# Attention scores in 32 x 64 tiles of the array, and half of the x3 tiles turned through DRAM

## The chip, the cores and the metric

The kernel runs on one core of a Trainium2 chip. The metric is the time of one execution on the device in microseconds (us). Engines are named as in the profile: PE is TensorE's matrix product, PEld its load of weights, DVE is VectorE, ACT ScalarE, POOL GpSimd; SPq, POOLq and ACTq are the queues from which transfers (DMA) are issued.

## What is computed

A block of four layers over 8 x 512 tokens of 1024 features, all in f32, each with a layer norm ahead and a residual around it:

```
x = x + softmax_attention(layernorm(x))      # 32 heads of 32 features, no mask
x = x + gated_dense(layernorm(x))            # x1 -> x2
x = x + sigmoid_attention(layernorm(x))      # 4 heads of 256 features, causal: x2 -> x3
x = x + gated_dense(layernorm(x))            # same weights as above: x3 -> out
```

In softmax attention, q, k and v come from one product with `attn_qkvw`; `probs = softmax(q @ k.T / sqrt(32))`, `ctx = probs @ v`, then a product with `attn_ow`. In sigmoid attention q, k and v are the normed x itself times a vector of signs for each, and `attn = sigmoid(4 * scores / 16)` below the diagonal. The gated dense layer is

```
dots = softmax(x @ centroids.T / 0.1); hits = dots > 0.01       # 64 clusters
out = (x @ weight.T + bias) where any(hits, axis=1) and cluster_sel[assignments], else 0
```

so it has to know the cluster logits of all tokens, and which clusters any token hit, before its output is gated.

## The kernel before, in words

Work is cut into 32 tiles of 128 tokens (four to a batch). The order on every engine is written out by hand: instructions run on each engine in the order in which the program issues them, and semaphores follow from the tiles that they read and write. Every f32 product runs on PE as two passes, so the profile has two matmul records and two weight loads for each; a bf16 product has one.

Stage 1, softmax attention, goes over 64 units (batch by group of 4 heads, the loop `for n in range(units)` from line 1002). A unit has four score steps for the maxima of the next unit (`rows_step`, product at line 871, negated maximum on DVE at 872) and four for its own exponentials (`keys_step`: product of keys and queries at 900, subtraction of the maximum as a bf16 product with ones at 903, exponential on ACT at 905). A score step writes one PSUM tile `sc` of 128 x (4 heads x 512); there is one such buffer, so rows and keys steps take turns with DVE and ACT reading it. Each head has 32 features, so its product uses 32 rows of the array: the four heads stand in four row groups, with 128 columns each. The array is then cut into tiles of 32 rows by 128 columns ("32*128" in the profile). Between score steps PE runs pieces of other work from a queue (`filler`, taken by `between`): the projections to q, k, v and the output product, cut into column tiles of 64 or 32 by `product` (line 554, "128*64" and "128*32"). Values (`values_step`, 927) and denominators (`normalize`, 939) are in 128*32.

Stage 2 is the first dense layer (line 1236), in 128*128. At its end, each pair of x2 tiles is normed and turned (features to partitions) by `block_pieces`: a block transpose of 32 x 32 on DVE (line 294), then four transfers from SP's queue (line 300) which put the blocks at their places in DRAM in pieces of 128 bytes.

Stage 3, sigmoid attention, goes over 32 heads (`for s in range(heads + 1)`). A step of this loop issues: loads of xT for head s + 2 (`load_head`, line 1275, SP's queue), the scores of head s (line 1295, `csc`), the logits by token of an earlier tile (line 333), k of the next head (line 1287, ACT), a load of an x2 tile (line 1484, SP's queue), the turn of a finished x3 tile, the norm of the next one, the values of head s - 1 (line 1314, `o`, added to x by DVE at 1320), the cluster logits of the turned tile, and what was held back (`run_held`: the steps of the cluster softmax). From step 5 on, each step finishes one x3 tile's path by one stage: norm in one step, turn and cluster logits in the next, logits by token in the one after.

The turn of an x3 tile is `turn_pieces`: eight transposes on PE against the identity (line 277) into two PSUM tiles, two copies out of PSUM (line 279, one by DVE and one by ACT), and a store of the turned tile to DRAM from GpSimd's queue (line 1442), from where the second dense layer loads it. The cluster logits are `by_cluster` (line 325, 128*64: two halves of the features in two column tiles) with a copy to `lT` by ACT (329), and `by_token` (333) after that.

Stage 4 is the second dense layer, with out stored tile by tile.

Of the kernel before, what the change touches and what calls it, by code (L numbers as in the profile page):

```python
# [13 lines left out]
F32 = mybir.dt.float32  # L14
# [8 lines left out]
P = 128  # L23
B, S, H = 8, 512, 1024
NT = B * S
NC = H // P
TPB = S // P
NTILE = NT // P
# [5 lines left out]
HEADS_B, HD_B = 4, 256  # L34
SIG_SCALE = 4.0 * HD_B ** -0.5

NCL = 64
# [31 lines left out]
class Filler:  # L69
# [38 lines left out]
    def run(self, count):  # L108

        while self.queue and count:  # L110
            count -= self._run_one() > 0
# [193 lines left out]
class Clusters:  # L305
# [8 lines left out]
    def pieces(self, t, xT, later=None, width=NCL, product=None):  # L314

        nc, (b, i), st, ps_m = self.stage.nc, divmod(t, TPB), {}, self.stage.ps_m

        def by_cluster():  # L320
            acc = ps_m.tile([P, P], F32, tag="mm", name="logitsT")
            for c in range(NC):
                for j in range(NCL // width):
                    rows = ts(c % 2 * (NCL // width) + j, width)
                    nc.tensor.matmul(  # L325
                        acc[rows, :], self.cT[:, c, ts(j, width)], xT()[:, c, :], start=(c < 2), stop=(c >= NC - 2)
                    )
            st["lT"] = self.pool.tile([P, P], F32, tag="lT", name=f"lT_{self.name}_{t}")
            nc.scalar.copy(st["lT"], acc)

        def by_token():
            acc = ps_m.tile([P, NCL], F32, tag="mm", name="logits")
            (product or nc.tensor.matmul)(acc, st["lT"], self.stage.cst.twice, start=True, stop=True)
            if i == 0:
                self.logits[b] = self.pool.tile([P, TPB, NCL], F32, tag="lg", name=f"lg_{self.name}_{b}")
            nc.scalar.activation(self.logits[b][:, i, :], acc, AF.Copy, scale=INV_TEMP)
            if i == TPB - 1:
                steps = self.softmax(b)
                if later is None:
                    for step in steps:  # L340
                        step()
                else:
                    later(steps)

        return [(1.3, by_cluster), (0.25, by_token)]

    def softmax(self, b):

        nc, small, st = self.stage.nc, self.stage.small, {}
        lg = self.logits.pop(b)  # L350

        def wide(t):
            return t.unsqueeze(2).to_broadcast([P, TPB, NCL])

        def first():
            top = small.tile([P, TPB], F32, tag="top", name="top")
            nc.vector.tensor_reduce(top, lg, AX.X, ALU.max)
            nc.vector.tensor_tensor(lg, lg, wide(top), ALU.subtract)

        def exp():  # L360
            nc.scalar.activation(lg, lg, AF.Exp)

        def second():
            den = small.tile([P, TPB], F32, tag="cden", name="cden")
            nc.vector.tensor_reduce(den, lg, AX.X, ALU.add)
            nc.vector.reciprocal(den, den)
            nc.vector.tensor_tensor(lg, lg, wide(den), ALU.mult)

        def third():
            nc.vector.tensor_scalar(lg, lg, THRESHOLD, None, ALU.is_gt)  # L370
            nc.vector.tensor_reduce(self.query[:, ts(b, TPB)], lg, AX.X, ALU.max)

        def fourth():
            turned = lg.rearrange("p t c -> p c t")
            if b == 0:
                nc.vector.tensor_reduce(self.hits, turned, AX.X, ALU.max)
            else:
                some = small.tile([P, NCL], F32, tag="some", name="some")
                nc.vector.tensor_reduce(some, turned, AX.X, ALU.max)
                nc.vector.tensor_max(self.hits, self.hits, some)  # L380

        return [first, exp, second, third, fourth]

    def rows_pieces(self, one_hot, bias, pool, out):

        nc, ps_m, st = self.stage.nc, self.stage.ps_m, {}

        def count():
            acc = ps_m.tile([NCL, P], F32, tag="mm", name="count")
            nc.tensor.matmul(acc, self.hits, self.stage.cst.ones, start=True, stop=True)  # L390
            st["sel"] = self.pool.tile([P, P], F32, tag="lT", name="cluster_sel")[:NCL]
            nc.vector.tensor_scalar(st["sel"], acc, 0.0, None, ALU.is_gt)

        def rows():
            out["rows"] = pool.tile([P, H], F32, tag="rows", name=f"rows_{self.name}")
            out["bias"] = pool.tile([P, H], F32, tag="rbias", name=f"rbias_{self.name}")
            for half in range(2):
                cols = ts(half, S)
                acc = ps_m.tile([P, S], F32, tag="mm", name="sel")
                nc.tensor.matmul(acc, st["sel"], one_hot[:, cols], start=True, stop=True)  # L400
                nc.vector.tensor_copy(out["rows"][:, cols], acc)
            nc.vector.tensor_tensor(out["bias"], out["rows"], bias, ALU.mult)

        return [(0.3, count)], [(1.7, rows)]


def softmax_attention(tc, cst, stage, filler, clusters, pools, dr, late, args):
# [11 lines left out]
    nc, small, ps_m = tc.nc, stage.small, stage.ps_m  # L419
# [45 lines left out]
    used, side, tiles, waiting, ready, held = {"w": 0}, deque(), deque(), deque(), deque(), []  # L465
# [397 lines left out]
    def rows_step(n, qt):  # L863

        st = state[n]
        if qt == 0:
            st["nmax"] = small.tile([P, TPB, GH], F32, tag="nmax", name=f"nmax_{n}")
        sc = ps_s.tile([P, GH, S], F32, tag="sc", name="sc")
        for h in range(GH):
            rows = ts(h, HD_A)  # L870
            nc.tensor.matmul(sc[:, h, :], st["q"][rows, ts(qt, P)], st["k"][rows, :], start=True, stop=True)  # L871
        nc.vector.tensor_reduce(st["nmax"][:, qt, :], sc, AX.X, ALU.max, negate=True)  # L872

    def split_max(n):
# [19 lines left out]
    def keys_step(n, kt):  # L894

        st = state[n]
        sc = ps_s.tile([P, GH, S], F32, tag="sc", name="sc")
        for h in range(GH):
            rows = ts(h, HD_A)
            nc.tensor.matmul(sc[:, h, :], st["k"][rows, ts(kt, P)], st["q"][rows, :], start=True, stop=False)  # L900
        for h in range(GH):
            rows = ts(h, HD_A)
            nc.tensor.matmul(sc[:, h, :], cst.ones_h[rows, :], st["shift"][rows, :], start=False, stop=True)  # L903
        pT = ptp.tile([P, GH, S], F32, tag="pT", name=f"pT_{n}_{kt}")
        nc.scalar.activation(pT, sc, AF.Exp, scale=SCALE_A)  # L905
        st["pT", kt] = pT
# [95 lines left out]
    for n in range(units):  # L1002
# [33 lines left out]
        for i in range(TPB):  # L1036
# [13 lines left out]
            if i == 0 and n > 0:  # L1050
                values_step(n - 1, 1)
                if ready:
                    by_cluster, by_token = ready.popleft()
# [274 lines left out]
def block_body(tc, long, dr, args, out):  # L1328
    x, xT_in, qkvw, qkvb, ow, ob, bv_q, bv_k, bv_v, wT, fbias, cT, assign = args
    nc = tc.nc  # L1330
    cst = Consts(nc, long)
# [13 lines left out]
    small, lgp, ps_m = at_left("small", 2), at_left("lg", 1), at_left("ps_m", 3, PSUM)  # L1345
    stage, filler = Stage(tc, cst, small, ps_m), Filler()
    hits1 = Clusters(stage, long, lgp, cT_s, "a")
    hits2 = Clusters(stage, long, lgp, cT_s, "b")
# [38 lines left out]
    sel, pairs = {}, NTILE // 2  # L1387
# [72 lines left out]
            turns.append((scale, stage.block_pieces(xn, xT, dr.xT2[t])))  # L1460
        return turns

    def x3_pieces(t):

        xn, xT, last = turned_tile(t, dr.xT3)
        norm = stage.norm_pieces(lambda: x2[t], xn)
        norm.insert(1, (0.0, lambda: nc.gpsimd.dma_start(dr.x3[t], x2[t])))
        later = held.extend if t < NTILE - TPB else None
        return norm, stage.turn_pieces(xn, xT, last, vector=(t < NTILE - TPB - 1)), hits2.pieces(t, xT, later)


# [55 lines left out]


    sig.open(pools(sig_stack, left))
    turned, normed, by_token = None, None, []  # L1530
    for s in range(heads + 1):
        load_head(s + 2)
        if s < heads:
            sig.scores(*divmod(s, HEADS_B))
        run(by_token)
        by_token = []
        if s + 1 < heads:
            sig.keys(*divmod(s + 1, HEADS_B))
        if s == 0:
            for t in range(2, TPB):  # L1540
                sig.value(t, x2, keep(t))
        elif s == 1:
            run([scale for scale, _ in turns])
        load_x2(s + TPB)
        turned, normed = normed, None
        if turned is not None:
            run(turned[0])
        if s > HEADS_B:
            norm, *normed = x3_pieces(s - HEADS_B - 1)
            run(norm)  # L1550
        if s > 0:
            sig.values(*divmod(s - 1, HEADS_B), x2)
        if turned is not None:
            run(turned[1][:1])
            by_token = turned[1][1:]
        run_held()
        if s in (2, 3):
            run(turns[s - 2][1])
        t = s + TPB - 1
        if TPB <= t < NTILE:  # L1560
            sig.value(t, x2, keep(t))
# [88 lines left out]
```

## Time and profile before

| what | us |
|---|---|
| median of 3 runs | 3797.39 (3795.68 to 3800.85) |
| the profiled execution | 3800.22 |
| its span, first to last instruction | 3798.5 |

By stage, from the windows of the trace (busy time, us):

| stage | window | PE | DVE | ACT | POOL | DMA share |
|---|---|---|---|---|---|---|
| first norm and projections | 0 to 70 | 58.5 | 32.9 | 6.6 | 9.8 | 0.50 |
| softmax attention | 70 to 2580 | 2484.4 | 1728.0 | 667.0 | 376.9 | 0.51 |
| end of output product, dense 1 | 2580 to 3046 | 453.0 | 362.2 | 68.3 | 42.5 | 0.66 |
| sigmoid attention | 3046 to 3392 | 341.3 | 166.7 | 156.1 | 165.4 | 0.53 |
| dense 2 | 3392 to 3798 | 398.5 | 249.4 | 18.0 | 7.6 | 0.38 |

How such lines are read: a group of instructions is "line engine operation out<-in shape xcount", then its busy time and the mean of one in ns (matmuls overlap, so count times mean is more than busy), then the idle time of the engine just before them and who ended it. "128*64" is the cut of the array: rows by columns. A line of the timeline is "start, duration, engine, line, operation", with equal instructions that follow each other merged.

### The profile page before, as it was taken

What the parts mean: (1) busy time and instruction counts of PE and PEld (TensorE: products, weight loads), DVE (VectorE), ACT (ScalarE), POOL (GpSimd) and SP (SyncE); (2) the same over time, 40 slices, a digit from 0 to 9 for tenths busy, and PEclk for the clock granted to TensorE, in tenths of its full rate; (3) what the DMA queues carried; (4) which work ended last, traced back from release to release, by engine and by line L of the source; (5) the groups of instructions that cost most, each with busy time, mean ns of one, the idle gap of its engine ahead of it and who ended that gap; (6) DMA issues with size and microseconds to landing.
All of it is one profiled execution on the core that took longest, in us unless ns stands there. A gap on an engine that the chain in (4) does not pass through costs nothing.

```text
span 3798.5 us, 72361 instructions
## 1 busy us (share of the span) xinstructions
PE 3735.7 (98%) x30850; PEld 1914.9 (50%) x30850; DVE 2539.2 (67%) x3495; ACT 916.0 (24%) x996; POOL 602.2 (16%) x585
## 2 busy tenths in 40 slices
PE   8999999999999999999999999998999999999999
PEld 4444454544554555455445445543444467764444
DVE  4767676767667666766866767665788844456556
ACT  1222222222222222222222222232111144430000
POOL 1222111111111111111111111111000045530000
PEclk9999999999999999999999999999999999999999
DMA  5335455645655455465465454456566765543332
GB/s 169 114 126 170 130 144 148 191 137 146 189 145 146 151 174 149 131 198 148 131 182 152 144 149 121 120 158 226 155 177 177 188 178 193 193 186 133 128 133 100
DMA packets 674544, 591.47 MB, mean 156 GB/s; under 512 B 268072, under 2 KB 519984, under 8 KB 674224
## 3 DMA queue, kind: packets, MB, share of 16 engines
q1 hardware_dynamic: 645120, 482.77, 44.3%
q0 software_dynamic: 24784, 88.36, 5.9%
q10 hardware_dynamic: 4320, 15.73, 1.0%
q8 instruction: 244, 4.00, 0.5%
q14 instruction: 76, 0.62, 0.0%
HBM read 452.48 MB, written 134.25 MB: 154 GB/s over the span
## 4 chain that ended last, share of the span: by engine, by line
PE 90%; DVE 7%; issue 1%; DMA 1%; ACT 0%; POOL 0%; SPq 0%; DVEq 0%; ACTq 0%; POOLq 0%
PE mm L554 39%; PE dense L1236 19%; PE sc L900 7%; PE sc L871 7%; PE av L927 6%; PE csc L1295 4%; PE o L1314 4%; DVE nmax L872 2%; PE logitsT L325 1%; PE sc L903 1%; PE den L939 1%; PE tp L277 1%; DVE sum L916 1%; DVE ln_st L227 0%; DVE xT L534 0%
## 5 line engine op out<-in xcount | busy, mean ns | idle before, releaser
L872 DVE TENSOR_REDUCE nmax<-sc 128x4 f32<-128x2048 f32 x256 | 586.0, 2289 | 298.5 <-PE sc L871 298.5
L905 ACT ACTIVATE pT<-sc 128x2048 f32<-128x2048 f32 x256 | 480.8, 1878 | 1147.5 <-PE sc L903 1136.4
L554 PE MATMUL mm<-xT,w 128*64 128x256 f32 (+1 forms) x3736 | 429.4, 384 | 1.8 <-DVE rden L942 1.7
L914 POOL TENSOR_TENSOR sum<-pT,pT 128x1024 f32<-128x1024 f32 x128 | 309.7, 2443 | 753.4 <-ACT pT L905 712.2
L554 PEld LDWEIGHTS mm<-xT,w 128*64 128x64 f32 (+1 forms) x3736 | 242.2, 135 | 198.6 <-issue 46.5
L554 PE MATMUL mm<-s,w 128*32 128x256 f32 (+1 forms) x3672 | 321.3, 381 | 3.9 <-DVE qk L144 3.4
L900 PE MATMUL sc<-qk,qk 32*128 32x512 f32 x2048 | 294.0, 644 | 17.2 <-DVE nmax L872 16.4
L871 PE MATMUL sc<-qk,qk 32*128 32x512 f32 x2048 | 294.8, 640 | 0.5 <-ACT pT L905 0.3
L916 DVE TENSOR_TENSOR sum<-sum,pT 128x2048 f32<-128x2048 f32 x128 | 292.0, 2281 | 1.0 <-ACT pT L905 1.0
L142 DVE TENSOR_TENSOR u<-dense,u 128x512 f32<-128x512 f32 x223 | 149.2, 686 | 183.9 <-PE dense L1236 167.0
L554 PEld LDWEIGHTS mm<-s,w 128*32 128x32 f32 (+1 forms) x3672 | 179.9, 122 | 180.8 <-issue 64.2
L554 PE MATMUL mm<-ow,ctxT 128*32 128x512 f32 (+2 forms) x1276 | 246.4, 599 | 0.8 <-DMA ow<-o_T 0.8
L927 PE MATMUL av<-pT,v 128*32 128x512 f32 x2048 | 246.6, 599 | 0.0
L1236 PE MATMUL dense<-sum,s 128*128 128x512 f32 x512 | 232.2, 594 | 2.6 <-DVE s L1183 2.6
L554 PEld LDWEIGHTS mm<-w,xT 128*64 128x64 f32 (+1 forms) x3888 | 197.5, 133 | 57.2 <-issue 44.7
L554 PE MATMUL mm<-w,xT 128*64 128x128 f32 (+1 forms) x3888 | 218.1, 274 | 0.0
L144 DVE SCALAR_TENSOR_TENSOR qk<-mm,qkvb_s,qk 128x256 f32<-128x256 f32 x224 | 107.6, 480 | 123.7 <-PE mm L554 118.7
L554 PE MATMUL mm<-ow,c 128*64 128x512 f32 (+2 forms) x864 | 171.1, 597 | 2.8 <-DMA ow<-o_T 2.8
L1236 PE MATMUL dense<-wT_s,dT_b 128*128 128x512 f32 x384 | 171.4, 594 | 1.6 <-DMA dT_b<-xT 1.6
L1236 PE MATMUL dense<-wT_s,dT_a 128*128 128x512 f32 x384 | 171.1, 594 | 0.0
L554 PE MATMUL mm<-w,s 128*64 128x128 f32 x2688 | 162.5, 274 | 0.0
L1236 PEld LDWEIGHTS dense<-sum,s 128*128 128x128 f32 x512 | 96.6, 190 | 123.2 <-issue 111.9
(230 smaller groups left out, 4548.4 us busy)
## 6 DMA issues: line engine op xcount, KB each, us to landing
w<-in_qkvw SPq DMA_DIRECT2D x252, 256.0 KB, 3.0
ow<-o_T SPq DMA_DIRECT2D x240, 256.0 KB, 3.7
w<-qk_T SPq DMA_DIRECT2D x224, 256.0 KB, 2.8
ow<-in_ow SPq DMA_DIRECT2D x180, 256.0 KB, 3.2
w<-v_T SPq DMA_DIRECT2D x112, 256.0 KB, 2.7
x<-in_x SPq DMA_DIRECT2D x32, 512.0 KB, 4.6
dT_a<-xT SPq DMA_DIRECT2D x32, 512.0 KB, 6.1
x_a<-x SPq DMA_DIRECT2D x32, 512.0 KB, 6.7
```

The costliest lines, as they stand in the source:

```text
L142: nc.vector.tensor_tensor(out, acc, other, ALU.add)
L554: nc.tensor.matmul(out[cols], lhsT[:, cols], rhs, **flags)
L871: nc.tensor.matmul(sc[:, h, :], st["q"][rows, ts(qt, P)], st["k"][rows, :], start=True, stop=True)
L872: nc.vector.tensor_reduce(st["nmax"][:, qt, :], sc, AX.X, ALU.max, negate=True)
L900: nc.tensor.matmul(sc[:, h, :], st["k"][rows, ts(kt, P)], st["q"][rows, :], start=True, stop=False)
L905: nc.scalar.activation(pT, sc, AF.Exp, scale=SCALE_A)
L914: nc.gpsimd.tensor_tensor(st["sum"][:, h, :], st["pT", 0][:, h, :], st["pT", 1][:, h, :], ALU.add)
L916: nc.vector.tensor_tensor(st["sum"], st["sum"], st["pT", kt], ALU.add)
L927: nc.tensor.matmul(st["av"][rows, :], st["v"][:, kt, rows], pT[:, h, :], start=(kt == 0), stop=(kt == TPB - 1))
L1236: nc.tensor.matmul(st["acc"], st["left"][LEFT[k]][:, c, :], self.w[RIGHT[k]][:, c, :], start=(c == 0), stop=(c == half - 1),)
L1295: nc.tensor.matmul(sc[:, AT_OFF[i] : AT_OFF[i] + n], k[:, c, ts(i, P)], xT[:, c, i * P :], start=(c == 0), stop=(c == 1),)
L1314: nc.tensor.matmul(acc[:, j - jj, :], at[:, start : start + P], self.v[b * TPB + i][:, cols], start=(i == 0), stop=(i == j),)
```

## The change

Three edits that can be told apart, and one of space:

1. Scores. In `rows_step` and `keys_step` each head's product of 128 columns becomes two of 64, which write the lower and the upper 64 partitions of the same place in `sc`; the product of the maxima with ones likewise. The array is then cut 32*64, in eight tiles. Products per rows step: 8 for 4; per keys step: 8 f32 and 8 bf16 for 4 and 4.
2. x3's even tiles, 0 to 24 (13 tiles), are turned by `block_pieces` in place of `turn_pieces`: the block transpose on DVE and its four sends from SP's queue are put behind what is held at the end of the step that normed the tile; in the next step a fetch from SP's queue brings the turned tile back from DRAM.
3. The cluster logits of an even tile then wait for those of the next odd tile, and both run one behind the other; so do their logits by token, one step later.
4. `lT` gets two buffers (`lT0`, `lT1`) for this, and the little tile `some` moves to another pool with one buffer in place of two.

```diff
@@ Clusters @@
-            st["lT"] = self.pool.tile([P, P], F32, tag="lT", name=f"lT_{self.name}_{t}")
+            st["lT"] = self.pool.tile([P, P], F32, tag=f"lT{t % 2}", name=f"lT_{self.name}_{t}")
...
-                some = small.tile([P, NCL], F32, tag="some", name="some")
+                some = self.pool.tile([P, NCL], F32, tag="some", name="some")
...
-            st["sel"] = self.pool.tile([P, P], F32, tag="lT", name="cluster_sel")[:NCL]
+            st["sel"] = self.pool.tile([P, P], F32, tag="lT0", name="cluster_sel")[:NCL]
@@ rows_step @@
-            nc.tensor.matmul(sc[:, h, :], st["q"][rows, ts(qt, P)], st["k"][rows, :], start=True, stop=True)
+            for j in range(2):
+                cols = ts(2 * qt + j, P // 2)
+                nc.tensor.matmul(sc[ts(j, P // 2), h, :], st["q"][rows, cols], st["k"][rows, :], start=True, stop=True)
@@ keys_step @@
-            nc.tensor.matmul(sc[:, h, :], st["k"][rows, ts(kt, P)], st["q"][rows, :], start=True, stop=False)
+            for j in range(2):
+                cols = ts(2 * kt + j, P // 2)
+                nc.tensor.matmul(sc[ts(j, P // 2), h, :], st["k"][rows, cols], st["q"][rows, :], start=True, stop=False)
...
-            nc.tensor.matmul(sc[:, h, :], cst.ones_h[rows, :], st["shift"][rows, :], start=False, stop=True)
+            for j in range(2):
+                cols = ts(j, P // 2)
+                nc.tensor.matmul(sc[cols, h, :], cst.ones_h[rows, cols], st["shift"][rows, :], start=False, stop=True)
@@ x3_pieces @@
-    def x3_pieces(t):
+    def x3_pieces(t, blocks=False):
...
+        if blocks:
+            made = []
+            def box():
+                if not made:
+                    made.append(Tpool.tile([P, NC, P], F32, tag="T3", name=f"B3_{t}"))
+                return made[0]
+            def fetch():
+                nc.sync.dma_start(xT().rearrange("p c t -> p (c t)"), dr.xT3[t])
+            held.extend(what for _, what in stage.block_pieces(xn, box, dr.xT3[t]))
+            return norm, [(0.0, fetch)], hits2.pieces(t, xT, later)
@@ the loop over heads @@
+    def in_blocks(t):
+        return t % 2 == 0 and t < NTILE - TPB - 3
...
-            norm, *normed = x3_pieces(s - HEADS_B - 1)
+            t = s - HEADS_B - 1
+            norm, *normed = x3_pieces(t, in_blocks(t))
...
-            run(turned[1][:1])
-            by_token = turned[1][1:]
+            clustered.append(turned[1])
+            if not in_blocks(s - HEADS_B - 2):
+                for by_cluster, _ in clustered:
+                    run([by_cluster])
+                by_token = [second for _, second in clustered]
+                clustered = []
```

`block_pieces`, which both x2's turn and this one call:

```python
def turn():
    self.nc.vector.transpose(box().rearrange("p c t -> p (c t)"), x())

def send():
    blocks = box().rearrange("p c t -> p (c t)")
    dst = dram.rearrange("(j q) (c i t) -> i q c j t", j=n, c=NC, i=n)
    for i in range(n):
        self.nc.sync.dma_start(dst[i], blocks[ts(i, 32)].rearrange("q (c j t) -> q c j t", c=NC, j=n))
```

More of the change, by code (lines that the diff above doesn't have):

```diff
@@ L1529, in block_body @@
     sig.open(pools(sig_stack, left))
-    turned, normed, by_token = None, None, []
+    def in_blocks(t):
+        return t % 2 == 0 and t < NTILE - TPB - 3
+    turned, normed, by_token, clustered = None, None, [], []
     for s in range(heads + 1):
```

## The prediction

> **What bounds the kernel now.** I read the page's parts 1, 2 and 4 first.
>
> ```profile
> PE 3735.7 (98%) x30850; PEld 1914.9 (50%) x30850; DVE 2539.2 (67%) x3495; ACT 916.0 (24%) x996; POOL 602.2 (16%) x585
> ...
> PEclk9999999999999999999999999999999999999999
> ...
> PE 90%; DVE 7%; issue 1%; DMA 1%; ACT 0%; POOL 0%; SPq 0%; DVEq 0%; ACTq 0%; POOLq 0%
> PE mm L554 39%; PE dense L1236 19%; PE sc L900 7%; PE sc L871 7%; PE av L927 6%; PE csc L1295 4%; PE o L1314 4%; DVE nmax L872 2%; PE logitsT L325 1%; PE sc L903 1%; PE den L939 1%; PE tp L277 1%; DVE sum L916 1%; DVE ln_st L227 0%; DVE xT L534 0%
> ```
>
> TensorE at full clock is the bound nearly everywhere; no other engine is near. So a change is worth what it takes off TensorE's own sequence. Next, do the scores wait for anyone (part 5)?
>
> ```profile
> L900 PE MATMUL sc<-qk,qk 32*128 32x512 f32 x2048 | 294.0, 644 | 17.2 <-DVE nmax L872 16.4
> L871 PE MATMUL sc<-qk,qk 32*128 32x512 f32 x2048 | 294.8, 640 | 0.5 <-ACT pT L905 0.3
> ```
>
> Hardly: 17.7 us of waits in 512 score steps (2048 records are 256 steps of 4 heads and 2 passes, since each f32 product runs as two). What is left is what a step costs by itself, in the timeline of TensorE's matmuls (PE) and weight loads (PEld):
>
> ```profile
> 1501.28 0.31 PEld L871 LDWEIGHTS sc<-qk,qk 32*128 32x128 f32 x8 [0.81 <-ACT pT L905]
> 1501.28 1.14 PE L871 MATMUL sc<-qk,qk 32*128 32x512 f32 x8
> ...
> 1502.35 0.20 PEld L554 LDWEIGHTS mm<-ow,ctxT 128*64 128x64 f32 x4 [0.76 <-issue]
> 1502.35 2.80 PE L554 MATMUL mm<-ow,ctxT 128*64 128x512 f32 x12
> ```
>
> A step takes 1.07 us (1501.28 to 1502.35). Its two passes stream 0.427 us each (second passes start 0.427 after the first ones stream), 0.853 together. The other 0.217 I took from the single records. The four loads start at 1501.278, .285, .291 and .298, one per 6.7 ns; the second set of loads starts at .387, so a load of 128 columns holds its square for 0.107, and nothing streams meanwhile. The last pass of the last head starts at .833, ends at 1502.260, and the next line's load comes at 1502.349: 0.089 of draining. So: load 0.107, staggered starts 3 x 0.0067 = 0.020, streaming 0.853, drain 0.090. For the 64-column work behind it the first load holds from 1502.351 to 1502.404: 0.053. A load not covered costs by its columns.
>
> **Scores in squares of 32 x 64.** Per step: load 0.107 becomes 0.053 (64 columns), seven staggered starts 0.047 instead of 0.020, streaming and drain as before. Sum 1.043 against 1.070: -0.027, by 256 + 256 steps = **-13.8 us**. In key steps the bf16 shift products (L903) go from 4 to 8 with the same stagger, already counted; their loads run under the f32 pass before them. Nothing else moves: bytes, exponentials and maxima are the same.
>
> This needs three things the trace shows only in part. (a) Both halves of a row group load and stream at once. Pairs of 128x64 and fours of 128x32 do so across columns (fours of 128x32 load in 0.027 and stream 8 products in 1.74), fours of 32x128 across rows; both together no row shows. Load bounds: 0.053, or 0.106 one after the other, which makes -13.8 into +13.4. I take the first, as the 128x64 pair loads two in 0.053. (b) Eight first passes overtake the second passes of earlier squares; the last is 26 records ahead of the oldest waiting one. Today's steps overtake by 10; but the queue is fed ahead: at 189 semaphore waits of TensorE's sequencer, 33 records before it had not yet started. (c) The stagger stays 6.7 ns. If it is hidden: -0.054 x 512 = -27.6; if it is 10 ns: -2.
>
> Does equal width (64 beside 64) spare the drain? These lines have equal width and unequal rows already:
>
> ```profile
> 41.00 5.42 PE L554 MATMUL mm<-xT,w_first 128*128 128x512 f32 x12
> 46.35 1.14 PE L871 MATMUL sc<-qk,qk 32*128 32x512 f32 x8
> 47.42 5.42 PE L554 MATMUL mm<-xT,w_first 128*128 128x512 f32 x12
> ```
>
> The score step again takes 1.07, and the pause before it, from the records, is 95 to 98 ns in all 5 such places, against 94 to 99 where rows and width both change. So no gain there.
>
> A rule speaks against the change: the Trainium skill, page "TensorEngine Tiling (Array Packing)", section "Instruction Overhead", gives each matmul some 60 cycles of overhead, which its page "TensorE: Matmul & The Clock Gate" puts at 25 ns of start-to-start floor. As an estimate from that, four more products a step would cost 0.100 us, and the scores would be 0.073 x 512 = 37 us slower. The trace's 6.7 ns between starts in different squares disagrees, and goes into the sum.
>
> **Even tiles of x3.** In the sigmoid stage (3046 to 3392 us) one head runs so:
>
> ```profile
> 3201.30 1.04 PE L277 MATMUL tp<-ident,n 128*128 128x128 f32 x8
> 3202.18 4.48 PE L1314 MATMUL o<-cn,at 128*128 128x256 f32 x20
> 3206.59 1.09 PE L325 MATMUL logitsT<-T,cT_s 128*64 128x128 f32 x16
> 3207.61 4.58 PE L1295 MATMUL csc<-cxT,k 128*128 128x512 f32 x16
> ```
>
> For 13 tiles (0, 2 to 24) the 8 transposes go: 3202.18 - 3201.30 = 0.88, **-11.4 us**. The even tile's cluster logits run right behind the odd one's turn, so 13 times one entry to and one exit from 128x64 go: 0.096 drain + 0.053 load, and 0.096 + 0.107, together 0.35: **-4.6 us**. TensorE really is the limit here, and the DMA engines have carried such blocks beside a full TensorE before (x2's turn, first row below, PE 100 of 100 us):
>
> ```profile
> 2850.00:2950.00 100.00, 100.00 (x235) 44.37 (x234) 79.58 (x110) 11.83 (x12) 7.26 (x12) 1.00 0.68 174
> 3140.00:3290.00 150.00, 150.00 (x857) 114.69 (x856) 74.05 (x170) 71.21 (x106) 74.95 (x107) 1.00 0.55 194
> ```
>
> What is added is off TensorE. VectorE gets a block transpose, 1.24, and loses a 0.69 copy, at half load; ScalarE loses a 0.58 copy. GpSimd loses a 512 KB store. SP's queue gets four block sends and one fetch. 4096 packets of 128 bytes by 13.2 ns (the packets' mean) over 16 engines are 3.4 us more per two heads of 10.9, so the DMA share goes from 0.55 to about 0.7, the first row's. The latency has a row, the same route in the attention stage:
>
> ```profile
> 1501.27 1.24 DVE L294 STREAM_TRANSPOSE nB<-n 128x1024 f32<-128x1024 f32 x1
> ...
> 1503.91 3.05 SPq L300 DMA_DIRECT2D xT<-nB  x4
> ...
> 1509.48 0.33 SPq L852 DMA_DIRECT2D nT<-xT  x1
> ```
>
> From the turn to the fetch 8.2, and the fetch lands 4.7 later (page, nT<-xT): 13 us. The turn starts some 1.6 us after the last product of its head (after four adds of 0.35), so the tile is there 14.6 after it. The logits come after the next head (4.42 + 0.34 + 4.41) and the scores, transposes and values of the one after (4.42 + 0.88 + 4.42): 18.9. Cover: 4 us. Behind the waiting send and fetch in SP's queue stand the loads of a head's xT and of x2, needed 10 us or more later by ScalarE's k (L1287) and the norm; they are issued over a head ahead. If the cover were gone, what is late is TensorE's logits, and with them csc.
>
> The second lT buffer and the moved `some` I cost at nothing: the logits wait 1.2 us on lT_a and 0.4 on lT_b in all, which VectorE and ScalarE hide; gone, at most 1.6 back.
>
> **Sum.** -13.8 - 11.4 - 4.6 = -29.8. The profiled run took 3800.2 (span 3798.5 and 1.7 around it): 3770.4. The median shown is 2.8 lower, so against it 3767.6. A tenth of the span being VectorE's on the chain, little is lost there: the 12 waits on nmax may grow by under 1 us.
>
> **Rivals.**
> - *The second halves start a pass late* (b fails): four squares run as today, four 0.427 later. Per step +0.427 - 0.027 = +0.400, x 512 = +205; with -16 from x3: 3986, slower. It decides as soon as over 16 of a step's 32 records must be looked through. For: nothing deeper than 10 is seen overtaken. Against: 33 queued.
> - *Loads of a row group's halves in turn*: +13.4 - 16.0 = -2.6: 3795. For: no row has two weights in one row group of 32. Against: 128x64 pairs.
> - *Starts wider apart*: in 128x32 fillers of 128 columns starts come 27 ns apart, which streaming explains. If it were a floor, 7 x 27 + 53 = 242 instead of 127 per step, +59 - 16: 3840. The skill's rule on overhead would be this one.
> - *The drain is spared at equal width*: 759 changes to or from 128x64 by 0.095: -72 more: 3696. The five places above speak against it; the tiling page of the Trainium skill says, too, that a change of mode drains, and the trace agrees (94 to 99 ns).
> - *The fetch comes late*: landing 9 instead of 4.7 (the longest xT landings in the trace are 9 to 10) would eat the 4 us and delay the logits 0 to 2 us, 13 times: x3's part then lies between -16 and +10, the time between 3768 and 3794, 3781 in the middle.
>
> **How the numbers follow.** Forecast 0.67 (own range 3753 to 3782: A -27.6 to -2, x3 -16 to -13); second halves late 0.10; loads in turn 0.08; starts apart 0.04; drain spared 0.04; fetch late 0.07. Range 3752 to 3798: forecast, loads in turn and late fetches, 0.8. A measurement of this kernel can tell about 0.2% (7.6 us) from no change. Faster: 0.67 + 0.04 + 0.06 of the late fetches = 0.77; same: loads in turn and the latest fetches, 0.09; slower: 0.10 + 0.04 = 0.14.
>
> **What would show it.** Right: a score step of 1.04 us in the timeline, x16 records, loads of mean about 0.13; 95 ns pauses unchanged; L277 down by 104 records, logitsT in runs of 32 records; heads without transposes about 9 us; no wait of logitsT on the fetch. Wrong: a step of 1.1 (loads in turn), of 1.45 (second halves late), pauses below 50 ns, or TensorE waiting for T<-xT.

## The result, and the profile after

| kernel | median us | runs | ratio to before, 95% interval |
|---|---|---|---|
| before | 3799.12 | 4 (3795.68 to 3801.16) | |
| changed | 3777.04 | 4 (3772.77 to 3777.33) | 0.9942 [0.9926, 0.9958] |
| changed, once more (`c0`) | 3778.07 | 5 (3770.63 to 3780.17) | 0.9947 [0.9934, 0.9959] |

The change makes the kernel 20 to 22 us faster, where 29.8 was forecast. The profiled execution's span went from 3798.5 to 3775.6, 22.9 less. First the page: engines, instruction queue, and the two groups of scores (names, then busy time and mean ns, then idle time before and its releaser).

```profile
PE 3710.4 (98%) x35866; PEld 1873.0 (50%) x35866; DVE 2545.7 (67%) x3495; ACT 909.8 (24%) x983; POOL 594.1 (16%) x572
...
q8 instruction: 283, 4.64, 0.5%
...
L904 PE MATMUL sc<-qk,qk 32*64 32x512 f32 x4096 | 286.8, 616 | 18.4 <-DVE nmax L874 17.4
...
L873 PE MATMUL sc<-qk,qk 32*64 32x512 f32 x4096 | 285.4, 613 | 0.6 <-ACT pT L911 0.3
```

PE is still the bound, with 5,016 more matmul records and 25 us less busy time. The instruction queue moved 283 pieces; before, it read:

```profile
q8 instruction: 244, 4.00, 0.5%
```

Now a rows step of the changed kernel in the timeline (start, duration, engine, line, operation):

```profile
1505.50 0.23 PEld L873 LDWEIGHTS sc<-qk,qk 32*64 32x64 f32 x16 [0.20 <-issue]
1505.50 1.11 PE L873 MATMUL sc<-qk,qk 32*64 32x512 f32 x16
1506.55 0.53 PEld L554 LDWEIGHTS mm<-w,xT 128*64 128x64 f32 x10 [0.81 <-issue]
```

The step is 1.05 long (1505.50 to 1506.55) where it was 1.07. Over all steps the medians, from the single records, are 1.044 for 1.071 (rows) and 1.260 for 1.287 (keys): the forecast's 0.027 to the nanosecond, in nearly all of the 256 steps of each kind. The starts stand 6.7 ns apart, the first load holds for 0.053, and the pauses at a change of form are the same before and after: 94 ns ahead of a score step and 89 behind it, in the median.

A pair of heads in the sigmoid stage:

```profile
3180.63 4.48 PE L1301 MATMUL csc<-cxT,k 128*128 128x512 f32 x16
3184.95 1.04 PE L277 MATMUL tp<-ident,n 128*128 128x128 f32 x8
3185.82 4.48 PE L1320 MATMUL o<-cn,at 128*128 128x256 f32 x20
3190.23 1.97 PE L325 MATMUL logitsT<-T,cT_s 128*64 128x128 f32 x32
3192.13 4.58 PE L1301 MATMUL csc<-cxT,k 128*128 128x512 f32 x16
3196.55 0.55 PE L333 MATMUL logits<-twice,lT_b 128*128 128x64 f32 x4
3196.94 4.54 PE L1320 MATMUL o<-cn,at 128*128 128x256 f32 x20
3201.31 1.02 PE L1301 MATMUL csc<-cxT,k 128*128 128x512 f32 x2
```

Two heads take 20.68 (3180.63 to 3201.31); before they took 2 x 10.91. Of the 1.13 saved the turn is 0.88, and 0.25 is left for the pairing. There are 13 such pairs. The window of the stage's middle (busy time of each engine, granted clock, DMA share) still has PE full, and DMA at 0.76 where it was 0.55:

```profile
3140.00:3290.00 150.00, 150.00 (x839) 115.65 (x838) 81.86 (x178) 73.30 (x106) 75.34 (x107) 1.00 0.76 230
```

The route of one tile, and the logits that use it:

```profile
3193.10 1.24 DVE L294 STREAM_TRANSPOSE B<-n 128x1024 f32<-128x1024 f32 x1
...
3194.36 3.00 SPq L300 DMA_DIRECT2D xT<-B  x4
...
3202.43 0.33 SPq L1485 DMA_DIRECT2D T<-xT  x1
```

From the turn to the fetch 9.3 us (forecast 8.2; 7.0 to 9.3 over the 13 tiles), and the logits start at 3210.92: nothing waits for T<-xT. Over the 13 tiles the logits start 8.5 to 12.2 us after the fetch is issued. The four fetches whose landing the trace has took 3.1 to 6.9, where the forecast had 4.7, so if the tightest tile's fetch took as long as the longest of these, 1.6 us of cover were left of the 4 forecast.

Where the 22.9 us came from, by comparing the starts of the same products in both traces: the sigmoid stage's first scores start 9.6 earlier (the shorter score steps alone are worth 13.5), the stage adds 15.5 up to its last scores, which makes 25.1, and 2.2 go back after them, 1.7 of it at the start of dense 2. That loss is one stretch of 3.4 us at half the granted clock, which follows a wait of 1.6 us for the first dT_b; the wait is there before too (1.56), but there the clock stayed.

Why 9.6 and not 13.5? The two traces run the same pieces of work between the same score steps, so each can be compared with its like. Among the pieces that no half-clock stretch touches, 31 became 0.04 to 0.15 longer. Here is one of them, after and then before (start, duration, engine, line, operation, wait):

```profile
1243.95 1.04 PE L945 MATMUL den<-sum,ones 128*32 128x512 f32 x8
1245.27 1.93 PE L554 MATMUL mm<-s,w 128*32 128x256 f32 x32 [0.28 <-DVE qk L144]
```

```profile
1248.16 1.04 PE L939 MATMUL den<-sum,ones 128*32 128x512 f32 x8
1249.35 1.93 PE L554 MATMUL mm<-s,w 128*32 128x256 f32 x32
```

From the first line to the second 1.32 us after and 1.19 before: PE comes sooner and waits for VectorE's qk. In 28 of the 31 the record that comes late waits for VectorE: for qk (L144) in 12, for the next maxima (L874) in 11, for `parts` (L884) in 5. Four other pieces became longer by 0.2 to 1.3, 2.0 us in all; they are the subject of c0. What the long steps of before give (2.5) and what half-clock stretches take (2.1) about cancel.

### The profile page after: what moved, and what is told of

Read it like the earlier page. It is cut to its first block, busy times and chain, and to the rows that moved or that the text cites. A ratio compares the mean times of both kernels' runs of the same rounds, so it can differ in the third digit from the quotient of the medians.

```text
span 3775.6 us, 82438 instructions
## 1 busy us (share of the span) xinstructions
PE 3710.4 (98%) x35866; PEld 1873.0 (50%) x35866; DVE 2545.7 (67%) x3495; ACT 909.8 (24%) x983; POOL 594.1 (16%) x572
## 4 chain that ended last, share of the span: by engine, by line
PE 88%; DVE 8%; issue 2%; DMA 1%; ACT 0%; POOL 0%; SPq 0%; DVEq 0%; POOLq 0%; ACTq 0%
PE mm L554 39%; PE dense L1242 19%; PE sc L904 7%; PE sc L873 6%; PE av L933 5%; PE o L1320 4%; PE csc L1301 3%; DVE nmax L874 2%; PE sc L909 1%; PE logitsT L325 1%; PE den L945 1%; DVE sum L922 1%; PE tp L277 1%; DVE xT L534 1%; DVE ln_st L227 1%
## 5 line engine op out<-in xcount | busy, mean ns | idle before, releaser
L874 DVE TENSOR_REDUCE nmax<-sc 128x4 f32<-128x2048 f32 x256 | 585.9, 2289 | 298.5 <-PE sc L873 298.4
L904 PE MATMUL sc<-qk,qk 32*64 32x512 f32 x4096 | 286.8, 616 | 18.4 <-DVE nmax L874 17.4
L873 PE MATMUL sc<-qk,qk 32*64 32x512 f32 x4096 | 285.4, 613 | 0.6 <-ACT pT L911 0.3
L144 DVE SCALAR_TENSOR_TENSOR qk<-mm,qkvb_s,qk 128x256 f32<-128x256 f32 x224 | 107.5, 480 | 121.9 <-PE mm L554 117.0
```

The costliest lines, as they stand in the source:

```text
L873: nc.tensor.matmul(sc[ts(j, P // 2), h, :], st["q"][rows, cols], st["k"][rows, :], start=True, stop=True)
L904: nc.tensor.matmul(sc[ts(j, P // 2), h, :], st["k"][rows, cols], st["q"][rows, :], start=True, stop=False)
```

## The experiments

All times below are against runs of the kernel before on the same chip. Record counts (a matmul or a weight load each) are those of the program.

**c0: the changed kernel again.** No edit.

> The changed kernel once more, unedited. Its first profile was 22.9 us shorter in span than the one of before, 7 less than forecast. Theory 1 (clock windows): TensorE's granted clock fell to half in 9 windows of 3.4 us in that profile and in 6 in the one of before; each costs about 1.7 us, and where they fall is a matter of phase. Then the profile's time follows its count of windows: 6 windows give a span of about 3770.5, 9 about 3775.6, and the median against before is about -25. Theory 2 (the gain is really 22): the span stays at 3774 to 3777 whatever the count, and the median at -21 to -23.

Median 3778.07 against 3798.13, -20.1. The profile has 6 stretches at half clock ahead of the last instructions, like the one of before, and its span is 3776.4, no shorter than the one with 9. So theory 1 falls as it stands: fewer half-clock stretches did not make the time shorter. They do cost what it says. Matched with the trace of before, the attention stage is 2.1 us longer inside the stretches in the first profile and 3.2 shorter in this one; but outside them the first is 11.5 shorter and this one only 5.3. What took the difference in this profile is mostly PE waiting on "issue", for nothing that the profile shows:

```profile
468.86 3.06 PE L554 MATMUL mm<-w,xT 128*64 128x128 f32 x52
473.09 1.17 PE L554 MATMUL mm<-w,xT 128*64 128x128 f32 x12 [1.17 <-issue]
```

The same 64 records ran without a break before (473.31, 3.71 long). Summed over the profile (who waited for whom: us in total, times, longest), c0 has:

```profile
PE mm L554 <- issue: 4.0, 4, 1.4
...
PE sc L873 <- issue: 0.4, 1, 0.4
```

Before shows no such wait by that name, though it has a stall of the same look inside one rows step, which lasted 2.64 us at 796.77 instead of 1.07.

**e1: scores alone.** The three score products of the change on the kernel before.

```diff
+            for j in range(2):
+                cols = ts(2 * qt + j, P // 2)
+                nc.tensor.matmul(sc[ts(j, P // 2), h, :], st["q"][rows, cols], st["k"][rows, :], start=True, stop=True)
```

> Scores in 32 x 64 squares, x3 as before. Theory 1 (load and stagger arithmetic): every score step 1.044 and 1.260 us instead of 1.071 and 1.287, 512 steps -13.7; about 2 us given back where TensorE waits for VectorE (maxima, q and k sums), so -11 to -12 at equal clock windows, plus or minus 1.7 for each window more or less. Theory 2 (the step gains but the queue behind it suffers from twice the records): clearly less than -9 at equal windows.

Median 3791.34 of 11 runs, ratio 0.9982 [0.9973, 0.9990]: -6.8. Its profiled run has steps of 1.044 and 1.260, only 3 half-clock stretches, none of them in the attention stage, and a span of 3784.8, 13.7 shorter. That this is the forecast's 13.8 is a coincidence. Matched with the trace of before, the attention stage is 13.2 shorter, of which 4.6 lie inside half-clock stretches that this run didn't have. Outside them the steps are 16.2 shorter (2.9 of it long steps that before has) and the pieces between them 7.5 longer, together -8.6. The median's interval is -10.3 to -3.8. So the steps gain what they should, and in the median half of it arrives. That is on theory 2's side: what is lost is lost between the steps.

**e2: x3 alone.** The change with the old score products.

> Even tiles of x3 through DRAM and paired logits, scores as before in 32 x 128. Theory 1 (TensorE work removed, all else hidden): the sigmoid stage 15 us shorter, score steps 1.071 and 1.287, so -15 at equal clock windows, and with e1 the two add up to the whole within 2 us. Theory 2 (part of the loss sits in x3's route, in SP's queue or the end of the stage): -11 or less.

Median 3784.5, ratio 0.9963 [0.9949, 0.9977]: -13.6, against 15 expected. The interval, -19.4 to -8.7, doesn't part the theories; the trace does. From the sigmoid stage's first scores to its last it has 309.6 us, as after the whole change, and before 325.2: theory 1. With e1 it adds up to -20.4, the whole's -20.1. The gap to the forecast lies in the scores' part.

**e7 and e9: fewer records.** All work between score steps in 128 columns, with the new scores (e7, 51,728 records) and the old ones (e9, 41,488).

```diff
-        width[0] = form
+        width[0] = P
```

> The changed kernel with the work between score steps in 128 columns instead of 64 and 32: TensorE's records fall from 71,736 to 51,728, and the first load behind a score step rises from 0.053 to 0.107. Theory 1 (only loads, stagger and waits count): some 380 entries by +0.047 and some 250 by +0.06, so 20 to 35 us slower than the changed kernel. Theory 2 (TensorE is at times short of instructions, more so with more records): the stalls of 0.2 to 1.7 us inside fillers and score steps go, 3 to 8 us of them, so slower by less than that.

> As e7_filler128, with scores in 32 x 128 as before (41,488 records). With so few records nothing is short of instructions in either. Theory 2 (the scores' gain of 13 us is there, and half of it is lost to a short supply of instructions): e7 is 12 to 14 us faster than this. Theory 1 (the squares give 7 us on the clock whatever the supply): e7 is 5 to 9 us faster.

e7 took 3815.21 (1.0045 [1.0031, 1.0059]), e9 3827.82 (1.0084 [1.0071, 1.0098]). Neither profile has a wait on issue anywhere, and the steps are again 1.044 and 1.071. Between the medians lie 12.6 us, as theory 2 said; but the two profiled spans differ by 7.5 only (3818.0 and 3825.6). Matching the two traces settles it: in the attention stage, outside half-clock stretches, e7's steps are 13.5 shorter and its pieces 2.5 longer, together -11.0, near theory 2's 12 to 14. The rest of the difference between the spans lies in half-clock stretches, of which e7 has six ahead of the end and e9 five, and outside the stage. e7's +38 over the changed kernel is a little above theory 1's 20 to 35 for wider first loads. Against the trace of the changed kernel 473 pieces are longer, by 50.0 us, and 15 with stalls shorter, by 4.7: the stalls go, as theory 2 said, and that pays far less than the loads cost.

**e6: more records.** The same place, 32 columns: 99,368 records.

```diff
-        width[0] = form
+        width[0] = HD_A
```

> The changed kernel with all work between score steps in 32 columns: 99,368 records. Theory 1 (loads and stagger alone): entry 0.027 + 0.020 instead of 0.053 + 0.007, 380 times -0.013, 5 us faster than the changed kernel. Theory 2 (supply of instructions): stalls of over 1 us in many fillers of 128-column rows, 15 us slower or worse.

3817.23, ratio 1.0051 [1.0037, 1.0065]: 40 us slower than the changed kernel, where loads and stagger promise 5 faster (and 482 pieces without stalls are indeed 4.0 shorter). Waits on issue in its profile:

```profile
PE mm L554 <- issue: 26.3, 14, 3.9
```

Stalls of up to 3.9 us, and 15 half-clock stretches ahead of the end, several of them just behind such stalls. Theory 2, clearly: PE stalls, and the more records the work is cut into the more it does. Over the profiles the sum of waits on issue goes with the records: 0 (41,488, 51,728 and 61,704), 0.5 (61,496), 1.9 (67,016, e11 below), 0.6 to 6.7 (71,500 to 71,900, five kernels in six profiles), 11 (92,216), 27 (99,368). These sums leave out stalls that stand inside a score step: before and e2 have long rows steps, most at the same places as the stalls, 2.9 and 2.8 us too long in all, and e7 and e9 have none.

That instructions are what PE is short of is shown for part of e6 only. Nine of its 16 waits on issue end 2.4 to 2.6 us after a transfer of the instruction queue starts, and these come every 9.6 us. Of c0's five waits none ends so. And e6, e7 and e9 change the width of the products together with their number. What runs short in the changed kernel stays open.

**e11: fewer records only where the stalls stood.** Pieces between score steps that hold v products alone, in 128 columns.

```diff
-        width[0] = form
+        next_up = filler.ahead()
+        width[0] = P if form > HD_A and next_up and all(w == 0.9 for w in next_up) else form
```

(`ahead` lists the weights of the pieces that the next `take` will run; 0.9 is a v product.)

> The changed kernel, and pieces between score steps that hold v products alone run in 128 columns: 67,016 records instead of 71,736, and 0.047 more for the first load of each such piece, some 90 of them. Theory 1 (loads alone): 4 us slower. Theory 2 (these pieces, with 128 columns streamed per product, are where TensorE runs out of instructions): no more waits on issue in the v pieces, which gives back 2 to 7 us, so from 2 slower to 3 faster.

3782.83, ratio 0.9957 [0.9945, 0.9970], 4.8 above c0's median, with intervals that overlap. The stalls in the v pieces are gone, one of 1.9 is left in a keys step; but the time is at theory 1's 4 us and not within theory 2's span. The 4 is luck: against c0's trace 91 pieces are 0.04 to 0.15 longer, 7.7 us in all, and seven with stalls are shorter by 6.1. So both theories have a part, and the loads cost more than the stalls give back. Less cutting there doesn't pay.

**e5: scores in 32 x 32.** Four column tiles per head.

```diff
-            for j in range(2):
-                cols = ts(2 * qt + j, P // 2)
+            for j in range(4):
+                cols = ts(4 * qt + j, P // 4)
```

(and so in the two products of `keys_step`, with 32 partitions of `sc` each)

> As the changed kernel, with scores in 32 x 32 squares: 16 per step. Theory 1 (first load by its columns, then 6.7 ns for each further square): load 0.027, 15 staggered starts 0.100, streaming 0.853, drain 0.090, a step of 1.070 as with 32 x 128; so the whole about 13 us slower than the changed kernel. Theory 2 (narrower is better, the load's columns alone count): 1.02 and 13 us faster. Theory 3 (64 records of a step are more than the queue looks through): steps of 1.3 or more, over 100 us slower.

3857.58, ratio 1.0158 [1.0144, 1.0172]: 80 slower than the changed kernel. The timeline has both kinds of step:

```profile
1500.50 1.14 PE L873 MATMUL sc<-qk,qk 32*32 32x512 f32 x32
1501.57 3.67 PE L554 MATMUL mm<-s,w 128*64 128x256 f32 x32
1505.17 1.14 PE L904 MATMUL sc<-qk,qk 32*32 32x512 f32 x32
1506.05 0.69 PE L909 MATMUL sc<-shift,ones_h 32*32 32x512 bf16 x16
1506.67 1.92 PE L933 MATMUL av<-pT,v 128*32 128x512 f32 x16
```

Rows steps take 1.07 (median 1.077, minimum 1.070): theory 1's sum, and 64 records of one step are not too many. Keys steps take 1.50 (1505.17 to 1506.67) instead of the 1.29 of theory 1: in the records, just one of the 16 bf16 loads starts under the f32 passes at once, and from the third product on each load follows the product before it, after 1506.24, so the shift products cost one pass of 0.213 more. 256 x 0.21 = 54 of the 80 us, beside the 13 that theory 1 had. Theory 1's size fell there, on a limit that eight squares do not reach (their eight loads start at 1501.13 to 1501.18, 0.43 ahead of their products). What limits it was not tried.

**e3: no pairs.** Each tile's logits one step after its norm.

```diff
-            if not in_blocks(s - HEADS_B - 2):
+            if True:
```

> The changed kernel with the cluster logits of each tile run as before, one step after its norm; even tiles still go through DRAM. The fetch then has one head less. Theory 1 (route 13 us from the turn; the logits of an even tile come 1.6 + 13 after a head's last product, and now are due after 8.9): TensorE waits some 5 us for T<-xT in each of 13 tiles, so the sigmoid stage is over 40 us longer than in the changed kernel, longer than before too. Theory 2 (the route is hidden anyway): it is 13 x 0.25 to 0.35, 3 to 5 us, longer.

One run: 3901.39, 104 slower than before. The waits in the sigmoid stage:

```profile
PE logitsT L325 <- DMA T<-xT: 84.6, 13, 7.8
```

6.5 us in each of 13 tiles, 5 expected, and in most of those tiles the clock falls to half for up to three stretches of 3.4 us. From its first scores to its last the stage has 431.4 us, 121.7 more than in the changed kernel; the 37 beside the waits, which theory 1 did not have, come with 35 such stretches. For one tile the turn starts at 3247.18, the fetch is issued at 3254.90 and PE goes on at 3262.47: 15.3 us, so the fetch landed within 7.6, against 4.7 in the forecast. Theory 1. The pairing, then, is first of all the head's delay that hides the route; its own saving is small beside that.

**e4: pairs alone.** All tiles turned on PE, logits in pairs.

```diff
-            norm, *normed = x3_pieces(t, in_blocks(t))
+            norm, *normed = x3_pieces(t)
```

> The changed kernel with all x3 tiles turned on TensorE as before; the cluster logits of even and odd tiles still run in pairs. The sigmoid stage then shows the pairs alone: by the forecast's arithmetic 13 x 0.35 = 4.6 us shorter than before, and 11.4 longer than in the changed kernel. By the changed kernel's own heads (a pair of heads 20.68 instead of 21.81, of which the transposes are 0.88) the pairs are worth 13 x 0.25 = 3.3.

One run: 3805.46, 6.0 above the median of before (3799.44). Both sizes missed. A pair of heads is 0.6 us longer than before, not 0.25 or 0.35 shorter, since the transposes now come right behind two logits and wait for the copy of them:

```profile
PE tp L277 <- ACT lg_b L336: 8.2, 12, 0.7
```

Without those 0.7 the pair would be worth 0.1. So pairing alone loses: from its first scores to its last the stage has 331.2 us, 6.0 more than before. Where the even turn is gone there is nothing to wait in that place. The stage is 21.6 us longer than c0's.

**e8: all tiles through DRAM.** Tiles 0 to 24, three buffers, logits one head late, no pairs.

```diff
-    xring, npool, Tpool = sb("c_x", 10), sb("c_n3", 2), sb("c_T3", 2)
+    xring, npool, Tpool = sb("c_x", 10), sb("c_n3", 2), sb("c_T3", 3)
...
-        return t % 2 == 0 and t < NTILE - TPB - 3
+        return t < NTILE - TPB - 3
...
+            wait = 1 if in_blocks(s - HEADS_B - 2) else 0
+            while len(clustered) > wait:
+                by_cluster, second = clustered.pop(0)
+                run([by_cluster])
+                by_token.append(second)
```

> The changed kernel with all tiles of x3 up to 24 through DRAM, not the even ones alone, a third buffer for the turned tiles, and each tile's logits one head late instead of in pairs. Theory 1 (the route of 13 us stays under a head's cover): 12 more turns off TensorE, -10.6, and the pairs' saving of 3 to 4 us lost: 7 us faster than the changed kernel. Theory 2 (SP's queue and the DMA engines, with twice the blocks, become the bound of this stage: per head some 7 us of issuing and a DMA share near 0.9): TensorE waits for T<-xT or cxT in many heads, and the kernel is slower than the changed one.

3797.33 of 11 runs, 0.9995 [0.9986, 1.0004]: no faster than before, 19 slower than the changed kernel. Its waits and its stage's window:

```profile
PE logitsT L325 <- DMA T<-xT: 14.6, 19, 1.9
```

```profile
3040.00:3380.00 340.00, 317.54 (x1625) 234.29 (x1624) 176.73 (x359) 141.89 (x197) 149.07 (x218) 1.00 0.83 219
```

DMA share 0.83, PE no longer full (317.5 of 340; 335.2 and a share of 0.72 in the changed kernel). In the traces the sigmoid stage is 9.3 us longer than in the changed kernel, from its first scores to its last, and what follows 3.2; another 7.0 is lost ahead of the stage, where the two kernels do the same work, to stalls and half-clock stretches. SP's queue is where the route gets longer. The turn of 3211.87 is done at 3213.11, but its sends start at 3216.76, behind the fetch of the tile before (3216.38). Fetches wait 6.5 us in all for sends to land, in six places, against 2.5 in one in the changed kernel, and most go out 5 to 6 us ahead of the logits. Theory 2 for the stage: not all tiles fit on this route as it is ordered. A number between 13 and 25 was not tried, nor which of queue and DMA engines is the limit.

## Why the prediction was right in kind and a third too large

- *Score step of 1.043 for 1.070.* Shown, as the sum of load, stagger, streaming and drain (steps of 1.044 and 1.260), and its terms once more by e5's rows steps, where 0.027 + 15 x 0.0067 makes the same 1.07 as 32 x 128.
- *(a) both halves at once, (b) eight passes overtaking, (c) stagger of 6.7 ns.* All three held; the rivals "second halves late", "loads in turn" and "starts wider apart" fall with them. The Trainium skill's 60 cycles per matmul ("TensorEngine Tiling (Array Packing)", section "Instruction Overhead") do not show between squares of a step: 6.7 ns each.
- *No drain spared at equal width.* Held: 94 ns from 128x64 to 32x64 and 89 back, as between 128x64 and 32x128.
- *-13.8 from the scores.* This is the step that failed, by its size: e1 has -6.8 in the median, half of it. The 0.027 are there in nearly all 512 steps, and two things go against them. First, waits on VectorE. The forecast gave them under 1 us, for the maxima alone; between the traces of before and after, 32 pieces between score steps became 0.04 to 0.15 longer, 2.4 us in all (30 and 2.2 in c0), and almost all of them wait for VectorE: where PE waits for it, coming sooner gains nothing. Second, stalls on issue, which the forecast didn't have: it counted products and loads by their time alone. The six profiles with the new scores and the old pieces show what is left of 13.8. Outside half-clock stretches their attention stage is shorter than in the trace of before by 11.5 (after), 5.3 (c0), 8.6 (e1), 8.3 (e3), 2.5 (e4) and 4.1 (e8): 6.7 in the mean, as e1's median has it. With no stalls on either side, e7 against e9, it is 11.0. So of the 7 us missing some 2.5 go to waits and some 4 to stalls; the split rests on one trace each of before and of e9. That such stalls grow with the records is shown (e6, e7, e9); what runs short is not.
- *The range.* That the time came out within the forecast's own 3753 to 3782 is in part luck: that range was made for another stagger, and the stagger came out as forecast. What took 7 us was not in it.
- *-11.4 from the turns.* Held: 0.88 for each of 13.
- *-4.6 from the pairs.* Too large: 0.25 a pair in place of 0.35, 3.3 us. The second logitsT saves 0.14 and the covered load of csc 0.10, as worked out. But o followed by csc in one form still takes 4.37, and 4.41 with a change behind it, so only 0.04 of the exit's drain came back; and two logits behind each other take 0.39, 0.05 more than twice one. And it is worth that only together with the turn's removal (e4).
- *The route hidden with 4 us of cover.* Held, with nothing waiting; e3 takes the cover away and pays 84.6 us of waits. In e8 most fetches go out 5 to 6 us ahead of the logits in place of 8.5 to 12.2, and 14.6 are paid. The load on the DMA engines came out at 0.76 for 0.7.

## What to carry to other kernels

Behind a change of the array's cut, the first weight load lies bare and costs by its columns, and each further tile costs a fixed stagger; the best cut is where the two together are least, here 64 columns (1.044) and neither 128 (1.071) nor 32 (1.070). Count the instructions that a finer cut adds, not their time alone: gains of tens of ns per step can be eaten by stalls of the bound engine that come with more instructions, and by waits on another engine that do not move. A transfer that replaces work of the bound engine is free only while it is issued far enough ahead, so move its user along with it, and stop before the queues fill.

## What the runs showed that was not expected

- PE stalls with nothing shown to wait for. The instruction queue's 244 pieces of 16 KB before and 283 after go with 61,704 and 71,736 records (about 253 to a piece); stalls of 0.2 to 3.9 us come with them. In the changed kernel, e1, e3, e4 and e8 they come at some or all of the same six places in every run, around 470, 790, 1115, 1435, 1755 and 2075, some 320 us apart, in or near the pieces with 64 short products `mm<-w,xT`; what changes from run to run is how long they are.
- 16 squares do well with f32 and not with the bf16 products behind them: 0.21 us more per keys step.
- The clock falls to half in stretches of 3.41 us, 6 to 9 of them ahead of the end in a profile of the changed kernel and of before, each worth about 1.7 us when PE is full; a wait of 1.6 us at a stage's start met one in the profile after and none before.
